# Conditioned transformer block on one core: early clearing of silu's tile, a sixth idle product, later ff gates, another bank for one modulation product

## The chip, the cores and the metric

The kernel runs on one core of one Trainium2 chip. The metric is the device time of one execution in microseconds (us); the lower, the better. The time before the change is the median of three runs.

## The reference

The input x has 2 batches of 2048 rows of 512 float32 numbers. A condition vector t of 512 numbers per batch gives six vectors per batch (shift, scale and gate, once for each of two halves of the block).

```python
emb = silu(t) @ ada_w + ada_b                  # (2, 6 * 512)
shift_msa, scale_msa, gate_msa, shift_mlp, scale_mlp, gate_mlp = split(emb, 6)
norm = ln(x) * (1 + scale_msa) + shift_msa
h = gelu(norm @ ssm_w1 + ssm_b1)               # exact gelu, 512 -> 512
x = x + gate_msa * (h @ ssm_w2 + ssm_b2)
norm2 = ln(x) * (1 + scale_mlp) + shift_mlp
hf = gelu_tanh(norm2 @ ff_w1 + ff_b1)          # 512 -> 1024
x = x + gate_mlp * (hf @ ff_w2 + ff_b2)
```

Everything is float32.

## The kernel before

**Tiles.** The 4096 rows are cut into 8 blocks of 512 rows, four to a batch. A block x_i lies in SBUF as 128 partitions x 4 pieces (c) x 512. Per block there are four large products: hA (norm times ssm_w1, class `First`), oA (times ssm_w2, added to x), hC in two groups (norm2 times ff_w1, class `Second`) and oC (times ff_w2, added to x).

**Seven products in place of eight.** Each large product is done as seven products of quarter matrices, P1 to P7 (function `group`). Their operands are quarters and sums of quarters: nS and hS for the activations, w_s and fw_s for the weights (`sums_of_first`, `sums_of_second`, four instructions each). The order is P1, P2, P6, P5, P7, P3, P4, and in the first blocks (`FIRST`) P1, P2, P5, P6, P7, P3, P4. P1, P6, P7 and P4 share one bank of PSUM, "y"; P2 has "x", P5 and P3 have "v". After a product, VectorE (DVE) takes its bank out, and only then may the next product with that bank be written.

**The order is written by hand.** `hook(hooks, places, ops)` hangs other work behind a product; it is issued on its engine right after that product's additions. [...]

**Pools.** PSUM has a pool `ps_g` with two buffers for each of the tags x, y and v, and a pool `ps_t` with two buffers of the tag t. A new tile takes the buffer of the tile of its tag before the last, and waits until that has been read.

**The start.** SP asks, in this order, for x_0, parts 0 and 1 of ada_w, w1, part 2, w2, x_1, parts 3 and 4, the row b2 (`b2_bc`), fw1, part 5, fw2 and the row fb2. Meanwhile TensorE (PE) does `IDLE` products whose result nobody reads, and turns the small rows (condition and biases) into columns, `colsT`. ScalarE (ACT) takes silu of the condition into a tile that GpSimd (POOL) has cleared, since only 2 of its 32 columns per piece are filled (lines 578 to 584). `ada_rows(g)` then makes part g of emb with four products side by side (pada, line 158), `modulation` turns it into a column per batch (pmod), and `gates` into a row on all partitions (pgate), whose result for batch 0 stays in a ps_t buffer and is multiplied into the second weights (`weight_of_second`, the folds at line 250) and into the bias row (line 629).

**Block 0 and 1.** The norm is x times rstd plus nmr (`normal`, ACT line 348 or DVE line 352), where the statistics come from DVE (lines 315 and 316, `stats`) and rstd and nmr from POOL (`scales`, lines 324 to 335). Then it is transposed on PE in pieces k = 0 to 3 (pt, line 377) and modulated (`modulate`: ACT line 391 or DVE line 393). Around the change, the order of PE is:

- hA_0, with pada_2 behind P2 and the gates of part 2 behind P6;
- oA_0, with pada_3 and pada_4 behind P2 (`conditioning`, which also issues the norm of block 1 on ACT), the two pmods behind P6, and pt_1_0 to pt_1_3 behind P7, P3, P4 and P4;
- hA_1, with pada_5 behind P6 and the transposes of the second norm of block 0 (pt_0_0 to pt_0_3) behind P3 and P4;
- the gates of part 5, and then hC_0, hC_1 and so on in the main loop.

On POOL, the biases of x (line 495), the sums of w2 and the scales of block 1 follow the multiplied row of line 629.

Of the kernel before, what the change touches and what calls it, by code (L numbers as in the profile page):

```python
# [36 lines left out]
F32 = mybir.dt.float32  # L37
# [6 lines left out]
def kernel(  # L44
# [16 lines left out]
    nc = tc.nc  # L61
    P = 128
    B, N, D = x.shape
    H = fw1.shape[1]
    KD = D // P
# [20 lines left out]
    out_blk = out.flatten_outer_dims().rearrange("(i p c) d -> i p c d", p=P, c=C)  # L86

    G = 32
    IDLE = 5


    R_COND, R_ADA = 0, B * KD
# [58 lines left out]
    load_row(b2_bc, b2)  # L151
    fw1_sb = load_w("fw1", fw1)

    def ada_rows(g, bias=None):

        pa = ps_g.tile([P, D], F32, tag="x", name=f"pada_{g}")
        for k in range(KD):
            nc.tensor.matmul(  # L158
                pa[k * G : (k + 1) * G, :],
                silu[:, k, :],  # L160
                ada[g][:, k, :],
                start=True,
                stop=True,
                tile_position=(0, k * G),
            )
        t = work.tile([P, D], F32, tag="tmp", name=f"adarows_{g}", bufs=4)
        if bias is None:
            nc.scalar.activation(t, pa, AF.Identity)
        else:
            nc.vector.tensor_tensor(t, pa, bias, ALU.add)  # L170
        return t
# [16 lines left out]
    gate = {}  # L188

    def gates(g, b, sums_g):  # L190

        pg = ps_t.tile([P, D], F32, tag="t", name=f"pgate_{g}_{b}")
        nc.tensor.matmul(pg, pick_bc[:, b, :], sums_g, start=True, stop=True)
        gate[g, b] = pg
        if b:
            gate[g, b] = work.tile([P, D], F32, tag="gate", name=f"gate_{g}_{b}", bufs=2)
            nc.scalar.activation(gate[g, b], pg, AF.Identity)
# [47 lines left out]
    def weight_of_second(w_sb, s, gt, engs):  # L245

        K = w_sb.shape[1]

        def fold(k):
            engs[k % len(engs)].tensor_tensor(w_sb[:, k, :], w_sb[:, k, :], gt, ALU.mult)  # L250

        ops = [lambda k=k: fold(k) for k in range(K)]
        lo, hi = w_sb[:, : K // 2, :], w_sb[:, K // 2 :, :]
        q = {
            "11": lo[:, :, : D // 2],
            "12": lo[:, :, D // 2 :],
            "21": hi[:, :, : D // 2],
            "22": hi[:, :, D // 2 :],
        }
        s = thirds(s)  # L260
        return second_operands(q, s), ops + sums_of_second(q, s, nc.gpsimd)
# [31 lines left out]
    def hook(hooks, places, ops):  # L293

        for n, op in enumerate(ops):
            hooks.setdefault(places[min(n, len(places) - 1)], []).append(op)
# [249 lines left out]
    def run(ops):  # L546
        for op in ops:
            op()
# [5 lines left out]

    minus_half = const.tile([P, C], F32, tag="minus_half", name="minus_half")
    nc.gpsimd.memset(minus_half, -0.5)

    unread = small.tile([P, C], F32, tag="unread", name="unread", bufs=1)
    nc.scalar.activation(unread, minus_half, AF.Silu)
# [4 lines left out]

    idle = ps_g.tile([P, C, P], F32, tag="v", name="idle")
    for n in range(IDLE):
        if n == IDLE - 1:
            nc.tensor.transpose(pt[:, :ROWS], rows, ident[:ROWS, :ROWS])
        nc.tensor.matmul(
            idle, ident, ident.unsqueeze(1).to_broadcast([P, C, P]), start=True, stop=True  # L570
        )
# [3 lines left out]
    nc.vector.tensor_copy(colsT, pt[:, :ROWS])  # L575


    silu = const.tile([P, KD, G], F32, tag="silu", name="silu")
    nc.gpsimd.memset(silu, 0.0)
    nc.scalar.activation(  # L580
        silu[:, :, :B].rearrange("p k b -> p b k"),
        colsT[:, R_COND:R_ADA].rearrange("p (b k) -> p b k", b=B),
# [40 lines left out]
    found = {}  # L623
# [22 lines left out]
    hook(hooks, ("P1",), [n1[1].scales] + hA_sums[:2])  # L646

    def conditioning():
        rows_3, rows_4 = ada_rows(3), ada_rows(4)
        for c in range(C):  # L650
            n1[1].normal(c, on_pe=True)
        found.update(shift=rows_3, scale=rows_4)

    hook(hooks, ("P2",), hA_sums[2:] + [conditioning])
    hook(hooks, ("P6",), [lambda: modulation(3, 0, found["shift"]), lambda: modulation(3, 1, found["scale"])])
    hook(hooks, ("P7", "P3", "P4"), n1[1].turned((3,)))
    n2 = {0: Norm(0, 2)}
    st = n2[0].stats()
    hook(hooks, ("P3",), st[:2])
# [1 line left out]
    fw1_ops, fw1_sums = weight_of_first("fw1", fw1_sb)  # L661
    run(fw1_sums)
    run(n1[1].summed(nc.vector))
    run(st[2:])

    hooks = {}
    hook(hooks, ("P1",), [n2[0].scales])
    hook(hooks, ("P2",), [lambda c=c: n2[0].normal(c, on_pe=True) for c in range(C)])
    hook(hooks, ("P2",), biases(1, gb[2]))
    hook(hooks, ("P6",), [lambda: found.update(rows=ada_rows(5, brows[:, 1, :]))])  # L670
    hook(hooks, ("P3", "P3", "P4", "P4"), n2[0].turned((1, 3)))
    hA[1] = First(1, n1[1].ops, hooks, FIRST)
    for b in reversed(range(B)):
        gates(5, b, found["rows"])
    fw2_ops, fw2_fold = weight_of_second(fw2_sb, fw2_s, gate[5, 0], (nc.vector,))
    n2_sums = n2[0].summed(nc.vector, nc.gpsimd)
    run(n2_sums[:2])
    fb2_bc = work.tile([P, D], F32, tag="gb", name="gb5_0", bufs=2)
# [1 line left out]
    load_x(2)  # L680
    gb[5] = fb2_bc

    def gb5_0():
        nc.vector.tensor_tensor(fb2_bc, gate[5, 0], fb2_bc, ALU.mult)

    first_hooks = {}
    hook(first_hooks, ("P1", "P2"), n2_sums[2:])
    hook(first_hooks, ("P6", "P5", "P7", "P3"), fw2_fold[:4])
    fold = None


    for i in range(NBLK):
        nxt, nx2, last = i + 1 < NBLK, i + 2 < NBLK, i + 1 == NBLK
        if nx2:
            n1[i + 2] = Norm(i + 2, 1)

        hooks = {} if i else first_hooks
        if nxt:
            hook(hooks, EARLY if i else ("P2",), hA[i + 1].summed(nc.gpsimd))
        if nx2:  # L700
            hook(hooks, ("P2", "P3", "P4"), n1[i + 2].stats())
        if fold:
            hook(hooks, ("P5", "P7"), fold[:2])
        hC = Second(i)
        hC.group(0, n2[i].ops, hooks)

        hooks = {}
        if nx2:
            hook(hooks, ("P1",), [n1[i + 2].scales])
            hook(hooks, EARLY, [lambda c=c: n1[i + 2].normal(c) for c in range(C)])  # L710
            hook(hooks, ("P7", "P3", "P3", "P4"), [lambda c=c: n1[i + 2].turn(c) for c in range(C)])
            hook(hooks, ("P4",), [n1[i + 2].move])
        hook(hooks, EARLY, hC.summed(0, nc.gpsimd))
        if i == 0:
            hook(hooks, ("P1", "P2", "P6", "P5"), fw2_fold[4:8])
            hook(hooks, ("P7",), fw2_fold[8:] + [lambda: gb5_0(), lambda: run(biases(0, gb[5]))])
        if fold:
            hook(hooks, EARLY, fold[2:6])
        hC.group(1, n2[i].ops, hooks)

        hooks = {}
        hook(hooks, EARLY, hC.summed(1, nc.gpsimd))
        if nxt:
            if nx2:
                hook(hooks, ("P7",), n1[i + 2].moved())
            if fold:
                hook(hooks, EARLY, fold[6:8])
                hook(hooks, ("P7",), fold[8:])
            n2[i + 1] = Norm(i + 1, 2)
            hook(hooks, ("P3", "P4"), n2[i + 1].stats())  # L730
            residual(f"oA_{i + 1}", i + 1, hA[i + 1], w2_ops, KD // 2, hooks)
        else:
            for p in EARLY:
                run(hooks.get(p, ()))
        fold = None

        hooks = {}
        if nxt:
            hook(hooks, ("P1",), [n2[i + 1].scales] + [lambda c=c: n2[i + 1].normal(c) for c in range(C)])
            hook(hooks, ("P2", "P2", "P6"), [lambda c=c: n2[i + 1].turn(c) for c in range(C)])  # L740
            hook(hooks, ("P6",), [n2[i + 1].move])
        if i + 3 < NBLK:
            hook(hooks, ("P6",), [lambda: load_x(i + 3)])
        refold2 = (i + 2) % PER_B == 0 and nx2
        if refold2:
            hook(hooks, ("P1",), [lambda: load_w("w2", w2, w2_sb)])
        if nx2:
            if refold2:
                gb[2] = gate_bias(gate[2, (i + 2) // PER_B], b2, "gb2_1")
            hook(hooks, ("P1", "P2"), n1[i + 2].summed(nc.gpsimd))  # L750
            hook(hooks, ("P2", "P6"), biases(i + 2, gb[2]))
        if nxt:
            hook(hooks, ("P3",), n2[i + 1].moved())
        hook(hooks, ("P3",), [lambda: store(i, 0)])
        residual(f"oC_{i}", i, hC, fw2_ops, KH // 2, hooks, last)
        if not last:
            store(i, 1)
        if nxt:
            run(n2[i + 1].summed(nc.gpsimd))

        refold5 = (i + 1) % PER_B == 0 and nxt
        if refold5:
            load_w("fw2", fw2, fw2_sb)
            gb[5] = gate_bias(gate[5, (i + 1) // PER_B], fb2, "gb5_1")
            fw2_ops, fold = weight_of_second(
                fw2_sb, fw2_s, gate[5, (i + 1) // PER_B], (nc.vector,)
            )
        hooks = {}
        if nxt:
            hook(hooks, EARLY, biases(i + 1, gb[5]))  # L770
        if refold2:
            w2_ops, w2_fold = weight_of_second(w2_sb, w2_s, gate[2, (i + 2) // PER_B], (nc.gpsimd,))
            hook(hooks, ALL, w2_fold)
        if nx2:
            hA[i + 2] = First(i + 2, n1[i + 2].ops, hooks)
        else:
            for p in ORDER:
                run(hooks.get(p, ()))
# [45 lines left out]
```

## Time and profile before

| what | value |
|---|---|
| runs | 629.41, 629.85, 634.3 us |
| median | 629.85 us |
| profiled execution, its own time | 633.62 us |
| its span, first to last instruction | 631.5 us |
| mean granted PE clock | 0.986 of full |
| PE, DVE, ACT, POOL busy | 97%, 46%, 28%, 57% |
| HBM read, written | 25.20 MB, 8.39 MB |

The profiled execution is one run, and its own time is 2.1 us more than its span. Engine names are those of the profile: PE for products, PEld for loading their weights, DVE, ACT and POOL, and SP, which issues most of the transfers. "x<-y" is the tile written and the tile read. In a wait line the figures are the total in us, how often, and the longest. In a line of a stretch stand its length, each engine's busy time with the number of instructions, the granted PE clock, the busy share of the DMA engines, and GB/s. A timeline line has start, duration, engine, line of the kernel and operation, and in brackets how long the engine stood idle before it and what ended that.

### The profile page before, as it was taken

What the parts mean: (1) busy time and instruction counts of PE and PEld (TensorE: products, weight loads), DVE (VectorE), ACT (ScalarE), POOL (GpSimd) and SP (SyncE); (2) the same over time, 40 slices, a digit from 0 to 9 for tenths busy, and PEclk for the clock granted to TensorE, in tenths of its full rate; (3) what the DMA queues carried; (4) which work ended last, traced back from release to release, by engine and by line L of the source; (5) the groups of instructions that cost most, each with busy time, mean ns of one, the idle gap of its engine ahead of it and who ended that gap; (6) DMA issues with size and microseconds to landing.
All of it is one profiled execution on the core that took longest, in us unless ns stands there. A gap on an engine that the chain in (4) does not pass through costs nothing.

```text
span 631.5 us, 7734 instructions
## 1 busy us (share of the span) xinstructions
PE 615.3 (97%) x2835; PEld 528.7 (84%) x2835; DVE 292.8 (46%) x492; ACT 176.1 (28%) x264; POOL 359.5 (57%) x376
## 2 busy tenths in 40 slices
PE   6999899999999999999999999999999999997997
PEld 2768688888888888888888888888888888886886
DVE  3486586534553355433455357533555233532321
ACT  2223513314422333214123324115223222012110
POOL 3277459949437457358957259976455383314430
PEclk8799999999999999999999999999999999999999
DMA  8951001042021501433020640224010400012001
GB/s 328 417 221 68 0 2 46 22 109 92 1 68 37 163 0 27 125 86 114 1 63 21 183 153 8 60 58 142 1 50 18 134 1 0 1 38 96 1 0 67
DMA packets 22057, 47.72 MB, mean 76 GB/s; under 512 B 4052, under 2 KB 4608, under 8 KB 21124
## 3 DMA queue, kind: packets, MB, share of 16 engines
q1 hardware_dynamic: 21936, 47.20, 23.6%
q8 instruction: 22, 0.36, 0.2%
q14 instruction: 15, 0.12, 0.1%
q10 hardware_dynamic: 84, 0.03, 0.0%
HBM read 25.20 MB, written 8.39 MB: 53 GB/s over the span
## 4 chain that ended last, share of the span: by engine, by line
PE 94%; DVE 2%; DMA 1%; POOL 1%; ACT 0%; issue 0%; DVEq 0%; SPq 0%
PE py_oC L278 18%; PE py_hC L278 17%; PE pv_hC L278 9%; PE py_oA L278 9%; PE pv_oC L278 9%; PE py_hA L278 9%; PE pv_oA L278 4%; PE px_oC L278 4%; PE pv_hA L278 4%; PE px_hC L278 4%; PE px_oA L278 2%; PE px_hA L278 2%; PE pada L158 1%; PE pt L377 1%; PE pmod L181 1%; DMA x<-in_x_dram 1%
## 5 line engine op out<-in xcount | busy, mean ns | idle before, releaser
L495 POOL TENSOR_TENSOR x<-x,gb 128x512 f32<-128x512 f32 x64 | 79.8, 1281 | 15.1 <-issue 15.1
L391 ACT ACTIVATE nT<-nT,mod,mod 128x512 f32<-128x512 f32 x52 | 38.1, 802 | 171.8 <-DMA nT<-blocks 159.9
L278 PE MATMUL py_hC<-nS,fw_s 128*128 128x256 f32 x256 | 61.3, 383 | 2.2 <-POOL nS L219 2.2
L217 POOL TENSOR_TENSOR nS<-nT 128x512 f32<-128x512 f32 x13 | 16.5, 1272 | 79.7 <-ACT nT L391 46.4
L348 ACT ACTIVATE nT<-x,nmr,rstd 128x512 f32<-128x512 f32 x52 | 38.7, 803 | 68.9 <-POOL nmr L335 68.9
L278 PE MATMUL py_oC<-fw_s,hSC 128*128 128x256 f32 x256 | 57.9, 379 | 0.0
L278 PEld LDWEIGHTS py_hC<-nS,fw_s 128*128 128x128 f32 x256 | 48.8, 191 | 9.3 <-POOL nS L219 2.6
L278 PEld LDWEIGHTS py_oC<-fw_s,hSC 128*128 128x128 f32 x256 | 48.6, 190 | 6.6
L482 DVE TENSOR_TENSOR x<-py_oC,x 128x512 f32<-128x512 f32 (+1 forms) x33 | 22.2, 672 | 60.5 <-PE py_oC L278 60.1
L324 POOL TENSOR_SCALAR ve<-mv 128x4 f32<-128x4 f32 x16 | 4.3, 268 | 75.7 <-DVE mv L316 69.2
L315 DVE BATCH_NORM_STATS2 st<-x 128x6 f32<-128x512 f32 x64 | 43.1, 674 | 5.1 <-DMA x<-in_x_dram 4.8
L207 POOL TENSOR_TENSOR hSC<-hClo 128x512 f32<-128x512 f32 x16 | 20.4, 1273 | 29.4 <-ACT hClo L431 29.4
L359 DVE STREAM_TRANSPOSE blocks<-nT 128x512 f32<-128x512 f32 x52 | 34.0, 688 | 5.7 <-ACT nT L348 5.7
L482 DVE TENSOR_TENSOR x<-py_oA,x 128x512 f32<-128x512 f32 x32 | 22.1, 691 | 26.5 <-PE py_oA L278 25.7
L278 PE MATMUL py_hC<-nT,fw 128*128 128x256 f32 x128 | 30.6, 381 | 1.3 <-ACT nT L391 1.3
L278 PE MATMUL py_hA<-nS,w_s 128*128 128x256 f32 x128 | 30.4, 381 | 0.9 <-DVE s1hA L436 0.9
L278 PE MATMUL pv_hC<-nT,fw 128*128 128x256 f32 x128 | 31.2, 388 | 0.0
L278 PE MATMUL py_oA<-w_s,hSA 128*128 128x256 f32 x128 | 30.3, 380 | 0.0
L278 PE MATMUL pv_hC<-nT,fw_s 128*128 128x256 f32 x128 | 30.2, 379 | 0.0
L278 PE MATMUL py_hC<-nS,fw 128*128 128x256 f32 x128 | 30.2, 379 | 0.0
L278 PE MATMUL px_hC<-nT,fw 128*128 128x256 f32 x128 | 30.2, 379 | 0.0
L278 PE MATMUL py_oC<-fw_s,hChi 128*128 128x256 f32 x128 | 29.2, 380 | 0.5 <-DVE x L482 0.5
(146 smaller groups left out, 1255.2 us busy)
## 6 DMA issues: line engine op xcount, KB each, us to landing
nT<-blocks SPq DMA_DIRECT2D x208, 64.0 KB, 2.0
out_dram<-x SPq DMA_DIRECT2D x15, 512.0 KB, 7.5
x<-in_x_dram SPq DMA_DIRECT2D x7, 1024.0 KB, 6.9
ada<-in_L_cond_ada_w_dram SPq DMA_DIRECT2D x6, 1024.0 KB, 11.9
fw<-in_L_cond_ff_w_dram SPq DMA_DIRECT2D x3, 2048.0 KB, 15.1
w<-in_L_cond_ssm_w_dram SPq DMA_DIRECT2D x3, 1024.0 KB, 6.8
x<-in_x_dram SPq DMA_DIRECT2D x2, 512.0 KB, 4.6
gb<-in_L_cond_ssm_b_dram SPq DMA_DIRECT2D x2, 256.0 KB
```

Source lines behind the costliest of these rows:

```text
L158: nc.tensor.matmul(pa[k * G : (k + 1) * G, :], silu[:, k, :], ada[g][:, k, :], start=True, stop=True, tile_position=(0, k * G),)
L181: nc.tensor.matmul(pv[:, n, :], sums_g[:, n * P : (n + 1) * P], pick, start=True, stop=True)
L207: lambda: eng.tensor_tensor(s[1], q["11"], q["21"], ALU.subtract),
L217: lambda: eng.tensor_tensor(s[1], q["22"], q["12"], ALU.subtract),
L278: nc.tensor.matmul(ps[b][:, j, :], lhs(p, j, k), rhs(p, j, k), start=(fresh and j == 0 and k == 0), stop=(p in ("P2", "P3", "P4") and k == ...
L315: nc.vector.bn_stats(st, xs[self.i][:, c, :])
L348: nc.scalar.activation(t, x_c, AF.Identity, bias=self.nmr[:, c : c + 1], scale=self.rstd[:, c : c + 1])
L359: nc.vector.transpose(self.bl[:, :, :, c, :].rearrange("p m k q -> p k m q"), self.nT[:, c, :].rearrange("p (k m q) -> p k m q", k=KD, m=C),)
L377: nc.tensor.transpose(pt[:, c * P : (c + 1) * P], self.xn[:, c, k * P : (k + 1) * P], ident)
L391: nc.scalar.activation(dst, src, AF.Identity, bias=shift, scale=scale)
L482: nc.vector.tensor_tensor(d, ps[BANK[p]][:, js], d, ALU.add)
L495: lambda c=c: nc.gpsimd.tensor_tensor(xs[i][:, c, :], xs[i][:, c, :], gb, ALU.add)
```

## The change

Six places are edited. The tile of silu is cleared on POOL right behind `minus_half`, ahead of the scales of block 0, instead of behind them. One more idle product is issued; the transposition of the rows stays behind the fourth, so that two stand behind it. The product of ada part 4 goes to a buffer of `ps_t` instead of the tag x of `ps_g`. The fourth modulation of block 1's first norm goes from DVE to ACT. The last two statistics of block 0's second norm move from in front of hA_1 to behind P1 of hA_1, ahead of the scales. The gates of part 5, and the making of the list of fw2's folds, move from in front of hC_0 to behind its P1. The folds themselves keep their places.

```diff
-    IDLE = 5
+    IDLE = 6
...
-    def ada_rows(g, bias=None):
-
-        pa = ps_g.tile([P, D], F32, tag="x", name=f"pada_{g}")
+    def ada_rows(g, bias=None, pa=None):
+
+        if pa is None:
+            pa = ps_g.tile([P, D], F32, tag="x", name=f"pada_{g}")
...
     nc.gpsimd.memset(minus_half, -0.5)
+    silu = const.tile([P, KD, G], F32, tag="silu", name="silu")
+    nc.gpsimd.memset(silu, 0.0)
...
-        if n == IDLE - 1:
+        if n == IDLE - 2:
             nc.tensor.transpose(pt[:, :ROWS], rows, ident[:ROWS, :ROWS])
...
-    silu = const.tile([P, KD, G], F32, tag="silu", name="silu")
-    nc.gpsimd.memset(silu, 0.0)
...
-        rows_3, rows_4 = ada_rows(3), ada_rows(4)
+        rows_3 = ada_rows(3)
+        rows_4 = ada_rows(4, pa=ps_t.tile([P, D], F32, tag="t", name="pada_4"))
...
-    hook(hooks, ("P7", "P3", "P4"), n1[1].turned((3,)))
+    hook(hooks, ("P7", "P3", "P4"), n1[1].turned())
...
-    run(st[2:])
...
-    hook(hooks, ("P1",), [n2[0].scales])
+    hook(hooks, ("P1",), st[2:] + [n2[0].scales])
...
-    for b in reversed(range(B)):
-        gates(5, b, found["rows"])
-    fw2_ops, fw2_fold = weight_of_second(fw2_sb, fw2_s, gate[5, 0], (nc.vector,))
+
+    def ff_gate():
+        for b in reversed(range(B)):
+            gates(5, b, found["rows"])
+        found["fw2"] = weight_of_second(fw2_sb, fw2_s, gate[5, 0], (nc.vector,))
+
...
+    def fold5(lo, hi):
+        return [lambda k=k: found["fw2"][1][k]() for k in range(lo, hi)]
...
+    hook(first_hooks, ("P1",), [ff_gate])
     hook(first_hooks, ("P1", "P2"), n2_sums[2:])
-    hook(first_hooks, ("P6", "P5", "P7", "P3"), fw2_fold[:4])
+    hook(first_hooks, ("P6", "P5", "P7", "P3"), fold5(0, 4))
...
-            hook(hooks, ("P1", "P2", "P6", "P5"), fw2_fold[4:8])
-            hook(hooks, ("P7",), fw2_fold[8:] + [lambda: gb5_0(), lambda: run(biases(0, gb[5]))])
+            hook(hooks, ("P1", "P2", "P6", "P5"), fold5(4, 8))
+            hook(hooks, ("P7",), fold5(8, 12) + [gb5_0] + biases(0, gb[5]))
...
+        if i == 0:
+            fw2_ops = found["fw2"][0]
```

## The prediction

> **What bounds the kernel now.** I read the page first, then the waits of PE (who it waited for), then the timeline of the first 80 us, and last the busy table over chosen stretches, whose third column from the right is the granted PE clock.
>
> ```profile
> span 631.5 us, 7734 instructions
> PE 615.3 (97%) x2835; PEld 528.7 (84%) x2835; DVE 292.8 (46%) x492; ACT 176.1 (28%) x264; POOL 359.5 (57%) x376
> PEclk8799999999999999999999999999999999999999
> ...
> PE pada L158 <- ACT silu L580: 3.2, 1, 3.2
> ...
> PE pada L158 <- DVE x L482: 1.4, 1, 1.4
> ...
> PE py_hA L278 <- DVE s1hA L436: 0.9, 1, 0.9
> PE pgate L193 <- ACT nT L391: 0.7, 1, 0.7
> ```
>
> PE is busy 97% of the span, and from 80 us to 570 us it waits for nobody. Only the start has waits that this change touches: the four shown, 6.2 us. The clock row says the start is also slow (8, 7). The stretches show how:
>
> ```profile
> 8.09:11.50 3.41, 0.43 (x2) 0.00 (x0) 0.88 (x7) 0.01 (x1) 2.67 (x9) 1.00 1.05 393
> 11.50:14.91 3.41, 2.43 (x11) 0.70 (x11) 0.85 (x2) 1.36 (x3) 0.58 (x1) 0.50 1.05 408
> ...
> 21.74:25.15 3.41, 3.41 (x13) 3.05 (x12) 2.44 (x5) 1.53 (x2) 0.00 (x0) 0.50 1.05 408
> 42.20:45.60 3.40, 2.03 (x19) 0.47 (x17) 3.37 (x4) 0.60 (x1) 3.24 (x3) 1.00 0.00 0
> ...
> 578.10:581.52 3.42, 1.26 (x6) 1.00 (x6) 0.69 (x1) 0.63 (x1) 3.26 (x3) 1.00 0.00 0
> 581.52:584.93 3.41, 3.41 (x10) 2.68 (x9) 0.69 (x1) 0.00 (x0) 3.41 (x4) 0.50 0.00 0
> ```
>
> After a stretch of 3.41 us with 0.43 us of PE work the clock halves, for four stretches (11.50 to 25.15); after one with 1.26 it halves for one; after one with 2.03 (the two pada products with the 1.4 us wait between) it stays full. So the 3.2 us wait for silu costs itself and then half speed through the whole first stage. The lines that price the steps, from the timeline and from the view of the tile ada:
>
> ```profile
> 11.25 0.20 POOL L579 MEMSET silu<- 128x128 f32 x1
> 11.49 0.22 ACT L580 ACTIVATE silu<-colsT 128x8 f32<-128x8 f32 x1 [3.47 <-POOL silu L579]
> 11.76 1.93 PE L158 MATMUL pada<-ada,silu 128*32 128x512 f32 x8 [3.24 <-ACT silu L580]
> ...
> 33.87 0.67 DVE L629 TENSOR_TENSOR gb<-pgate,gb 128x512 f32<-128x512 f32 x1
> 34.68 4.97 POOL L495 TENSOR_TENSOR x<-x,gb 128x512 f32<-128x512 f32 x4 [15.05 <-issue]
> ...
> 49.60 2.93 ACT L348 ACTIVATE blocks<-x,nmr,rstd 128x512 f32<-128x512 f32 x4 [2.75 <-POOL nmr L335]
> 53.19 0.60 PE L377 MATMUL pt<-ident,blocks 128*128 128x128 f32 x4
> ...
> DMA to landing us min/median/max: 7.2/11.9/15.4
> ```
>
> **The Trainium skill.** "TensorE: Matmul & The Clock Gate", Part 1, says that the array runs at half clock by default and after an idle window, at full clock after a busy one, that a window is 3413 ns, and that it runs free, so its phase differs from run to run. The trace agrees: the clock changes at 11.50, 25.15, 581.52 and 584.93 us, all whole multiples of 3.41 apart. That also explains two kinds of run: 629.41 and 629.85 against 634.3, the profiled one (633.62) being of the second kind. The same page, under "Architectural detail", has ACT, DVE and POOL as strict first-in-first-out queues; here px_oA's addition (L482), whose product had ended by 42.8, starts at 44.39, behind L207 and L208 on DVE. "DMA: Bandwidth & Descriptors", "Queues, rings and completion order": on each DMA engine descriptors are taken in ring order, so a row asked for behind nine large loads comes after them. The first four pieces of ada's landings agree (8.8, 11.6, 16.7, 24.3 us, in the order of issue).
>
> **Part 1, silu cleared early and a sixth idle product.** Before: nmr ends 11.31, memset 0.20, silu 0.22, pada at 11.76. After: POOL has nothing between 2.2 and 8.2 us, so the memset is free; silu follows colsT (ends 8.21) at about 8.27 and ends at 8.5. PE holds the second idle product behind rowsT: 0.86 us at full clock (two passes of 0.43, the spacing of the weight loads at 4.81 to 5.67), so it is free at 9.1. The first piece of ada lands at 1.63 + 7.2 = 8.8. So pada starts at 9.1 and takes 1.07 (the full-clock row at 27.69, against 1.93). ACT 0.60: 10.8; pmod 0.92 (half of 1.84 for x16): 11.7; second pada (its ada lands at 11.6): 12.8. The transposes now wait for nmr, unmoved at 11.31, plus two ACT normals of 0.75: 12.9. Then pt 1.0, pmod 0.95, pt 1.0: P1 of hA_0 at 15.8 instead of 23.14. Its w1 landed by 14.33. In the stretch 8.09 to 11.50 PE now has about 2.7 us of work, over the 2.03 that kept the clock, so I take the clock as full. For a run before with a full clock the same sum gives P1 at 18.45 and, with P1 at full speed as well (1.0 us), 5.7 us less than the profiled run; the runs show 3.8 to 4.9 less.
>
> **What is late next: b2.** L629 multiplies the row b2_bc by the gate. From P1 it comes 9.7 us later at full clock: 25.5. But b2_bc is asked for behind ada 4, whose issue began at 14.40 - 2.90 = 11.5 and landed 15.4 later, at 26.9; 256 KB at 410 GB/s add 0.6: 27.5. So DVE stands 2.0 us at L629. Queued behind it are the w2 folds and P7's addition; they had 1.0 us of room before P4, so PE stands about 1.0 there. POOL is the longer chain: from L629 its biases, the w2 sums and the scales lead to the end of ACT's normals at 52.53, 18.66 after L629. After: 27.5 + 18.66 = 46.2.
>
> **Part 2, own bank for ada part 4.** The 1.4 us wait for px_oA's addition goes: pada_4 follows pada_3. Its new slot was held by the ssm gate, last read by the folds (37.8 before, 31 after), 5 us ahead. But pt_1_0 needs the normals: PE would be there at about 44.1 and they end at 46.2. So pt_1_0 ends at 46.3 against 53.79: parts 1 and 2 give 7.5 us against the profiled run, 1.8 against a full-clock run (where pt_1_0 would end at 48.1). The bank alone is worth 0.6 of its 1.4, the slack between 52.53 and 53.19.
>
> **Part 3, hA_1: statistics behind P1's addition, fourth modulation on ACT.** L217 waits for ACT (59.72 instead of DVE's 59.41): +0.3. s1hA then starts at 62.6 instead of 63.92, and P6 at once at 63.74: 0.9 less. Back comes: the last aggregate ends 0.9 later, so nmr and the four normals end at 71.0 instead of 70.1, while pt_0_0 would now be reached at 70.4. Net 0.35 (bounds 0 and 0.9).
>
> **Part 4, the ff gates behind P1 of hC_0.** The 0.73 us wait for the transposes' bank is covered by P1 (1.73), which needs only modulations 0 and 1, done at 73.3. The two gate products cost 1.8 wherever they stand. ACT's gate copy and table load (0.6 + 1.28) end before P2's gelu. L219 comes 1 us before P6. Net 0.75 (bounds 0.4 and 0.9). The folds keep their places, and SP's queue its order.
>
> **Sum.** 7.5 + 0.35 + 0.75 = 8.6: the profiled execution (span 631.5, 2.1 around it, 633.62) would be 625.0. Against the two full-clock runs (mean 629.6): 1.8 + 0.35 + 0.75 = 2.9, or 626.7. My model makes the half clock about 1.2 us too dear, so I stand between: **626.0 us**, 0.6% under the median of 629.85. What a measurement of this kernel can tell from no change is about 1%, 6.3 us.
>
> **Rivals.**
> - *The row is no bound* (chance 0.11). If b2_bc lands by 25.5, L629 does not wait and pt_1_0 ends at 44.4: 1.9 less, 624.1. For: its landing is not shown, only worked out from ada's. Against: DMA is saturated (393 to 410 GB/s) up to 40 us.
> - *The new wait before pt_1_0 halves the clock once* (0.15). It empties about 2 us of a stretch; 3.4 - 2.0 = 1.4 us of work lies between 1.26 (halved) and 2.03 (kept). One stretch at half speed is 1.7: 627.7. For: 581.52. Against: the stretches have to fall on it.
> - *The first stage still runs at half clock* (0.12): pada and pmod may count for little (the stretches from 14.91 to 21.74 are full of such work and didn't raise the clock). Then P1 comes at 18.9, L629 at 29.7, 2.2 after the row: 628.2. Against: 42.20 to 45.60.
> - *Slower* (0.04): the new wait before pt_1_0 halves the clock, and the pieces of transposes there keep it so for four stretches, as from 11.50 to 25.15. Price 5.6: 631.6. It decides from 4 us lost on, three stretches. Against: P3 and P4 stand between those transposes, and the stretch with P1 in it (21.74) raised the clock.
>
> **Numbers.** Forecast 0.58, its own range 624.6 to 627.4. The range for 8 in 10 takes in the first two rivals and most of the third: 623.8 to 628.5. Faster by over 1% (below 623.6, or a comparison in which most runs before had the slow start): 0.17. Within 1%: 0.79. Slower by over 1%: 0.04, the last rival.
>
> **What would show it.** In the changed profile: silu near 8.3 and pada near 9.1 without a wait for ACT; clock 1.00 from 11.5 to 25; P1 of hA_0 near 16; L629 held by the DMA of gb near 27.5; a wait of about 2 us of pt for ACT's blocks near 46; no waits of pada for L482, of py_hA for s1hA, of pgate for nT. I am wrong if the clock is 0.50 in the first stage, if L629 starts near 25.5 without a DMA, or if hA_1 or hC_0 shows a new wait of over 1 us.

## The result and the profile after

Over ten runs of each, the changed kernel takes 626.92 us (624.87 to 627.35) and the kernel before 631.69 us (629.41 to 634.3). The ratio is 0.9918, with a 95% interval of 0.9893 to 0.9942: 0.8% faster, which is clear of no change but under 1%. The median of before rose from the 629.85 of its first three runs because most of the later runs were longer; what makes them so is the granted clock, as the part on the prediction works out. The profiled execution of the changed kernel has a span of 624.5 us and a time of its own of 626.36 us, against 633.62 us.

From the page of the changed kernel, the span, PE's busy time and the row of PE's clock:

```profile
span 624.5 us, 7738 instructions
PE 612.0 (98%) x2837; PEld 525.5 (84%) x2837; DVE 295.1 (47%) x491; ACT 176.5 (28%) x265; POOL 359.4 (58%) x376
...
PEclk9999999999999999999999999999999999998999
```

The clock's 8 and 7 at the start are gone. The 8 near the end is a stretch of half clock that before had too, at 581.52, spread there over two slices; it comes up again below. From the waits of PE in the changed kernel (who was waited for; total, times, longest):

```profile
PE py_hC L279 <- POOL nS L220: 2.2, 1, 2.2
PE py_hA L279 <- DVE s5hA L448: 1.5, 1, 1.5
...
PE pt L378 <- ACT blocks L349: 1.1, 3, 0.4
...
PE py_hA L279 <- DVE u2hA L443: 0.4, 1, 0.4
```

The four waits of before (pada for silu, pada for px_oA's addition, py_hA for s1hA, pgate for nT) are gone. Smaller ones have come in their place: P4 of hA_0 waits 1.5 us for an addition on DVE, the first transposes of block 1 wait 0.8 us for ACT and those of block 0's second norm 0.3 (1.1 in all), and P7 of hA_1 waits 0.4 us for P6's addition. The first line, 2.2 us, belongs to the last block and was there before. From the timeline of the changed kernel:

```profile
8.46 0.22 ACT L581 ACTIVATE silu<-colsT 128x8 f32<-128x8 f32 x1 [0.73 <-DVE colsT L578]
9.97 1.07 PE L159 MATMUL pada<-ada,silu 128*32 128x512 f32 x8
...
16.69 1.99 PE L279 MATMUL py_hA<-nT,w 128*128 128x256 f32 x8
...
29.17 0.69 DVE L630 TENSOR_TENSOR gb<-pgate,gb 128x512 f32<-128x512 f32 x1 [2.31 <-DMA gb<-in_L_cond_ssm_b_dram]
...
31.71 1.99 PE L279 MATMUL py_hA<-nS,w 128*128 128x256 f32 x8 [1.49 <-DVE s5hA L448]
...
44.84 2.93 ACT L349 ACTIVATE blocks<-x,nmr,rstd 128x512 f32<-128x512 f32 x4 [5.16 <-POOL nmr L336]
```

silu runs at once behind colsT, pada no longer waits and takes 1.07 us in place of 1.93, and hA_0 starts 6.5 us earlier. Then DVE stands 2.31 us for the transfer of the row b2: the row starts only 4.7 us earlier than before. From the view of the tile ada in the changed kernel, where the largest figure is that of part 4, asked for just ahead of the row (15.4 in before):

```profile
DMA to landing us min/median/max: 7.4/12.1/16.8
```

Part of what PE had gained beyond that goes into the new waits: P4 of hA_0 starts 5.7 us earlier (31.71 in place of 37.42).

### The profile page after: what moved, and what is told of

Its sections match the earlier page's. It is cut to its first block, busy times and chain, and to the rows that moved or that the text cites. A ratio compares the mean times of both kernels' runs of the same rounds, so it can differ in the third digit from the quotient of the medians.

```text
span 624.5 us, 7738 instructions
## 1 busy us (share of the span) xinstructions
PE 612.0 (98%) x2837; PEld 525.5 (84%) x2837; DVE 295.1 (47%) x491; ACT 176.5 (28%) x265; POOL 359.4 (58%) x376
## 4 chain that ended last, share of the span: by engine, by line
PE 92%; POOL 3%; ACT 1%; DVE 1%; issue 1%; DMA 0%; POOLq 0%; SPq 0%
PE py_oC L279 18%; PE py_hC L279 18%; PE pv_hC L279 9%; PE pv_oC L279 9%; PE py_oA L279 8%; PE py_hA L279 8%; PE px_oC L279 4%; PE pv_oA L279 4%; PE px_hC L279 4%; PE pv_hA L279 4%; PE px_oA L279 2%; PE px_hA L279 2%; PE idle L572 1%; ACT blocks L349 1%; PE pt L378 1%
## 5 line engine op out<-in xcount | busy, mean ns | idle before, releaser
L279 PE MATMUL py_oC<-fw_s,hChi 128*128 128x256 f32 x128 | 29.2, 380 | 0.5 <-DVE x L483 0.5
```

The source lines that it names most:

```text
L279: nc.tensor.matmul(ps[b][:, j, :], lhs(p, j, k), rhs(p, j, k), start=(fresh and j == 0 and k == 0), stop=(p in ("P2", "P3", "P4") and k == ...
```

## The experiments

All timelines can be set side by side at the same marks. The table gives the start in us of P1 of hA_0, of the multiplied row, of P3 of oA_0 (right behind pt_1_0), of P1 and P4 of hA_1, and of P2 of hC_0, and the time from there to the end of the span. It is one profiled execution each. The last two columns are the median and the ends of all runs, and the times of those runs whose mean granted clock is given as 1.000 ("full clock" below).

| kernel | hA_0 P1 | row | oA_0 P3 | hA_1 P1 | hA_1 P4 | hC_0 P2 | rest | runs: median (ends) | at clock 1.000 |
|---|---|---|---|---|---|---|---|---|---|
| before | 23.14 | 33.87 | 53.63 | 58.39 | 71.98 | 79.02 | 552.48 | 631.69 (629.41 to 634.3) | none |
| changed | 16.69 | 29.17 | 47.99 | 52.76 | 66.16 | 72.21 | 552.29 | 626.92 (624.87 to 627.35) | 624.87, 625.01 |
| p1_only | 16.24 | 28.98 | 47.80 | 52.57 | 66.59 | 73.63 | 553.07 | 628.29 (626.58 to 628.87) | 626.58 |
| warm_only | 20.11 | 29.94 | 49.69 | 54.46 | 68.05 | 75.08 | 552.92 | 627.28 (626.27 to 630.14) | 626.27, 626.71 |
| silu_late | 22.37 | 32.72 | 51.61 | 56.38 | 69.79 | 75.83 | 550.67 | 628.32 (627.27 to 628.37) | none |
| idle5 | 15.80 | 29.11 | 48.67 | 53.44 | 66.54 | 72.59 | 552.81 | 626.84 (626.62 to 627.24) | none |
| b2_late | 15.84 | 33.47 | 53.03 | 57.80 | 70.92 | 76.97 | 552.33 | 631.09 (629.8 to 632.47) | none |
| b2_early | 16.33 | 26.55 | 45.42 | 50.19 | 63.61 | 69.66 | 550.84 | 622.60 (622.4 to 624.12) | 622.40, 622.48, 622.73 |
| no_bank | 15.95 | 28.93 | 50.02 | 54.78 | 67.89 | 73.94 | 550.66 | 626.34 (624.86 to 628.96) | 624.86 |
| b2_early_no_bank | 16.85 | 26.75 | 46.50 | 51.27 | 64.36 | 70.41 | 551.09 | 623.14 (622.59 to 624.17) | 622.59, 622.87 |
| no_part3 | 16.67 | 29.12 | 47.93 | 52.70 | 66.70 | 72.75 | 550.55 | 625.63 (625.48 to 627.6) | 625.48, 625.59 |
| no_part4 | 16.74 | 29.21 | 48.02 | 52.78 | 66.19 | 73.22 | 550.68 | 626.89 (625.74 to 628.36) | 625.74, 625.79 |
| b2_scales | 16.86 | 26.84 | 45.05 | 49.82 | 63.25 | 69.30 | 552.30 | 621.80 (621.5 to 623.51) | 621.50, 621.58, 621.80 |
| b2_scales_idle5 | 17.34 | 27.16 | 45.40 | 50.17 | 63.60 | 69.65 | 552.95 | 623.38 (621.26 to 627.25) | 621.26, 621.55 |

The rest varies by 1.7 us with a stretch of half clock near the end that some executions have and others don't. Parts worth less than that are therefore read from the marks and from the runs at full clock, and not from the medians. The ratios below are to the runs of before that belong to each experiment. Their medians are 632.84 to 633.67, where the result above has 631.69, so these ratios are not to be set against each other.

**Part 1 alone, on the kernel before.**

```diff
-    IDLE = 5
+    IDLE = 6
...
     nc.gpsimd.memset(minus_half, -0.5)
+    silu = const.tile([P, KD, G], F32, tag="silu", name="silu")
+    nc.gpsimd.memset(silu, 0.0)
...
-        if n == IDLE - 1:
+        if n == IDLE - 2:
...
-    silu = const.tile([P, KD, G], F32, tag="silu", name="silu")
-    nc.gpsimd.memset(silu, 0.0)
```

> The kernel before with part 1 alone (silu's tile cleared early, sixth idle product). Theory (part 1 carries nearly all, through the silu wait and the clock): the clock is full from about 7 us on in every run, hA_0 starts near 16.7 us, the row of L629 waits for b2_bc near 29 us, and the time is 627.5 to 628.5 us with a spread under 2.5 us (the changed kernel less about 0.3 for pada_4's bank and 1.1 for parts 3 and 4). Rival (the later parts carry half): 629.5 us or more.

Measured: 628.29 us, ratio to before 0.9919 (0.9892 to 0.9946), within the expected band. The clock is full through the first stage, hA_0 starts at 16.24 and the row waits until 28.98 for its transfer. Part 1 carries 5.4 of the 6.8 us that hC_0's P2 moves (79.02 to 73.63, and on to 72.21).

**Eight idle products, silu still late.**

```diff
-    IDLE = 5
+    IDLE = 8
...
-        if n == IDLE - 1:
+        if n == IDLE - 4:
```

> The kernel before with eight idle products in place of five, four of them behind the transposition of the rows, and nothing else: silu stays late, so PE has work while it waits. Theory (the half clock costs 4 to 5 us, and the two kinds of run before differ by it): clock 1.00 in the first stage, hA_0 starts near 18.5 us in place of 23.1, all runs at 629.0 to 630.0 us, none near 634. Rival (the clock follows the late silu only, or its cost is covered by the wait for b2_bc): runs still spread from 629 to 634.

Measured: 627.28 us, ratio 0.9929 (0.99 to 0.9959), and better than expected: no run is near 634. So the half clock cost more than the expectation had put on it. The expectation took runs of 629 to 630 us for runs of before at full clock; the two runs here that had it took 626.27 and 626.71, no more than the 626.58 of p1_only. The expectation that the clock would be 1.00 throughout failed in the profiled run, the longest of the seven. PE's wait for silu is down to 0.6 us, and yet one stretch runs at half speed. The stretches before and after the change of clock (columns as in the prediction):

```profile
11.15:14.56 3.41, 2.12 (x19) 1.14 (x19) 1.00 (x2) 1.86 (x4) 0.43 (x3) 1.00 1.05 404
14.56:17.98 3.42, 3.42 (x17) 1.76 (x17) 0.17 (x1) 0.95 (x2) 3.26 (x3) 0.50 1.05 410
```

2.12 us of PE work did not keep the clock, though the kernel before kept it with 2.03 at 42.2. All but 0.06 of that work is pada (32 of 128 columns) and pmod (2 moving columns). In these records a stretch's busy time doesn't decide by itself.

**silu late in the changed kernel.** The two lines that clear silu's tile go back behind colsT; the sixth idle product stays.

> The changed kernel with silu's tile cleared late again, six idle products kept. Theory (one more product covers the wait only in part: PE is idle from about 9.4 to 11.8 us): the wait of pada for silu is 2 to 2.5 us, the clock may halve for one or more stretches between 11 and 25 us, hA_0 starts at 18.5 to 22 us, and with parts 3 and 4 kept the time is 627 to 630 us, more spread than the changed kernel. Rival (the clearing is worth nothing, since b2_bc bounds the start): 627 us with no half clock.

Measured: 628.32 us. PE waits 2.1 us for silu, and the clock is at half from 13.4 to 23.6:

```profile
9.97:13.38 3.41, 1.06 (x8) 0.16 (x8) 1.00 (x2) 0.60 (x2) 1.18 (x6) 1.00 1.03 389
13.38:23.62 10.24, 9.98 (x43) 8.07 (x44) 2.04 (x5) 3.74 (x6) 5.08 (x4) 0.50 1.04 413
```

hA_0 starts at 22.37 and hC_0's P2 3.6 us later than in the changed kernel. The median is 1.4 us higher; in the profiled execution 1.6 us of the 3.6 are made up in the rest, by the stretch at the end that it lacks. With six idle products the early clearing is what matters: one more product does not bridge the wait. Eight did so in most runs of warm_only, with silu still late. What counts is that DVE comes to the row by the time that b2 has landed, near 29, and the early clearing is one way to that.

**The sixth idle product undone.** `IDLE = 5`, one product behind the transposition.

> The changed kernel with five idle products, one behind the transposition of the rows (the sixth undone). Theory (silu is ready at 8.7 us and part 0 of ada_w lands at 9.0, so the sixth product only fills time): the first pada starts at 9.0 to 9.3 us, the clock is full until the wait for b2_bc, the row starts when it did, and the time is within 0.5 us of 626.9. Rival (the sixth product is what keeps the clock): half clock between 11 and 15 us, and 1 to 3 us more.

Measured: 626.84 us, no different from the changed kernel. pada starts at 9.10 (it waits 0.6 us for part 0 of ada_w) and hA_0 at 15.80, 0.9 us earlier, but the row starts at 29.11, as in the changed kernel: b2's transfer hides the sixth product. The clock is full through the first stage here too, without that product; behind the wait for the row it is at half for one stretch (31.9 to 35.3), and hA_1 starts 0.7 us later than in the changed kernel. What the sixth product is for shows only where that cover is gone, in b2_scales_idle5 below.

**The row b2 asked for earlier, and later.**

```diff
     load_x(1)
+    b2_bc = work.tile([P, D], F32, tag="gb", name="gb2_0", bufs=2)
+    load_row(b2_bc, b2)
     load_ada(3)
     load_ada(4)
-    b2_bc = work.tile([P, D], F32, tag="gb", name="gb2_0", bufs=2)
-    load_row(b2_bc, b2)
     fw1_sb = load_w("fw1", fw1)
```

> The changed kernel with the row b2_bc asked for ahead of parts 3 and 4 of ada_w. Theory (b2_bc's landing bounds the start): the multiplied row starts near 26.9 us in place of 29.2, PE's wait of 1.5 us at P4 of hA_0 is gone, the norm of block 1 ends 2.3 us earlier, and the time falls by 1.5 to 2.3 us, to 624.6 to 625.4. Rival (POOL's and ACT's chain has other bounds): the wait at P4 moves into the wait for the transposes of oA_0, and the time falls by under 0.5 us.

Measured: 622.60 us, ratio 0.9843 (0.9808 to 0.9878). The row starts at 26.55, behind the statistics on DVE and no transfer:

```profile
26.55 0.67 DVE L630 TENSOR_TENSOR gb<-pgate,gb 128x512 f32<-128x512 f32 x1
```

The wait at P4 is gone, pt waits 0.7 us in place of 1.1, and hC_0's P2 comes 2.55 us earlier (72.21 to 69.66), 0.3 over the upper end expected. The median falls by 4.3; 1.5 us of the difference between the two profiled executions is the half clock at the end, which this one lacks. At full clock three runs took 622.40 to 622.73 us, against 624.87 and 625.01: 2.4 us, as the marks say. In b2_late, the two lines stand behind fw1.

> The changed kernel with the row b2_bc asked for behind the 2 MB of fw1, which take about 5.1 us. Theory: the multiplied row starts near 34.2 us in place of 29.2, the wait at P4 of hA_0 grows by 5 us to 6.5, and the time rises by 5 us, to about 632, slower than before. Rival (the row is covered): under 1 us more.

Measured: 631.09 us over 20 runs, ratio to before 0.9981. The row starts at 33.47 and the wait at P4 is

```profile
PE py_hA L279 <- DVE s5hA L448: 6.4, 1, 6.4
```

as expected (6.5). The row moved by 4.3 us, hC_0's P2 by 4.8 and the median by 4.2. The wait also cost clock: it is at half from 32.5 to 39.3. So the landing of a 256 KB row bounded the changed kernel's start, in both directions.

**pada_4's bank undone**, with the row late and with it early: `ada_rows(4)` again.

> The changed kernel with the product of ada part 4 back in the tag x of ps_g (part 2 undone). Theory (the norm of block 1 bounds oA_0, so the bank is worth nothing while b2_bc is late): pada waits about 1.0 us for px_oA's addition again, the transposes no longer wait for ACT, pt_1_0 ends 19.0 us after the multiplied row starts, as with the bank, and the time is within 0.3 us of the changed kernel's 626.9. Rival (the prediction's 0.6 us): pt_1_0 ends 19.6 us after the row, 627.5.

Measured: 626.34 us. The profiled execution is no clean comparison: behind the wait for the row its clock halved for one stretch.

```profile
28.42:31.84 3.42, 1.44 (x7) 0.93 (x7) 2.91 (x5) 0.39 (x1) 2.08 (x2) 1.00 1.02 417
31.84:35.25 3.41, 3.41 (x10) 2.67 (x9) 2.91 (x7) 1.26 (x4) 3.41 (x4) 0.52 1.05 410
```

From the row to P3 of oA_0 it takes 21.09 us. With the bank and the same half clock (idle5) it is 19.56, with the bank and full clock (changed) 18.82, and without the bank and with full clock (p1_only) 18.82 too. So at full clock and with the late row the bank is worth nothing (the one run at clock 1.000, 624.86, says the same), and where half a clock has put PE behind, 1.5 us at that mark, from one trace each.

> The changed kernel with b2_bc early but pada_4 back in the tag x of ps_g. Theory (the bank saves PE time, but only what the norm of block 1 leaves): pada waits 1.0 to 2.0 us for px_oA's addition, the 0.7 us wait of the transposes goes, hA_1 starts 0.4 to 0.9 us later than with the bank (50.2), 623.2. Rival (worth nothing here too): within 0.2 us of 50.2.

Measured: 623.14 us. pada waits 1.4 us, and from the row to hA_1 it takes 24.52 us in place of 23.64: 0.9, at the upper end. The bank saves PE time, of which the norm of block 1 leaves a part, or none. By hC_0's P2 0.75 of it is left (70.41 against 69.66), and the two runs at full clock lie only 0.2 above those of b2_early, so how much of it reaches the time is not shown.

**Part 3 undone.** `turned((3,))`, and `run(st[2:])` back in front of hA_1.

> The changed kernel with the fourth modulation of block 1 back on DVE and the last two statistics back in front of hA_1 (part 3 undone). Theory from the two traces: P1 to P4 of hA_1 takes 14.0 us in place of 13.4, the time rises by 0.6 to 627.5. Rival (the prediction's 0.35, with the rest given back by the late norm): 13.75 us, 627.2. Second rival (part 3 costs, by the wait of the transposes for the norm): under 13.4.

Measured: hA_1 takes 14.00 us from P1 to P4 in place of 13.40, with a wait of 1.3 us for s1hA. hC_0's P2 is 0.5 later. The median of these four runs, 625.63, is 1.3 under that of the changed kernel all the same; the profiled one lacks the half clock at the end (1.7), so the medians don't settle a part of this size. At full clock two runs took 625.48 and 625.59 us, against 624.87 and 625.01: 0.6, as the marks say. Against before, the gain by the marks is less: there hA_1 took 13.59, with 0.9 of wait. In p1_only it takes 14.02 as well.

**Part 4 undone.** `ff_gate()` in front of hC_0.

> The changed kernel with the ff gates back in front of hC_0 (part 4 undone). Theory from the two traces: P4 of hA_1 to P2 of hC_0 takes 7.05 us in place of 6.05, PE waits 0.7 us for the fourth transpose's bank again, and the time rises by 1.0 to 627.9. Rival (the prediction's 0.75): 6.8 us, 627.7.

Measured: from P4 of hA_1 to P2 of hC_0 7.03 us in place of 6.05, with the wait back:

```profile
PE pgate L194 <- ACT nT L392: 0.7, 1, 0.7
```

The median is 626.89, and at full clock the two runs are 0.8 above those of the changed kernel. By the marks part 4 is worth 1.0 us: the 0.7 of the wait, 0.15 until the first gate product is under way, and 0.1 of the gates themselves, which take 1.71 us behind a running product and 1.82 behind a gap.

**A better version.** b2 early, and the scales of block 1 ahead of w2's last sum:

```diff
-    hook(hooks, ("P7",), fold2(2, 8))
+    hook(hooks, ("P7",), fold2(2, 7))
...
-    hook(hooks, ("P1",), [n1[1].scales] + hA_sums[:2])
+    hook(hooks, ("P1",), [n1[1].scales] + fold2(7, 8) + hA_sums[:2])
```

> The changed kernel with b2_bc asked for ahead of parts 3 and 4 of ada_w, and the scales of block 1 on POOL ahead of the last of w2's four sums (which P4 of oA_0 alone needs). Theory (with the row early, the norm of block 1 still ends 0.7 us behind PE): nmr ends 1.6 us earlier, the transposes don't wait for ACT, hA_1 starts at 49.4 to 49.6 us in place of 50.2, and the time is 0.6 to 0.8 us under the same kernel with the row alone (622.6), near 621.9. Rival (the last sum is late for P4, or POOL and DVE get in each other's way): no gain or a new wait at P4 of oA_0.

Measured: 621.80 us, ratio to before 0.9829 (0.9807 to 0.9852), the best of all. From the row to hA_1 it takes 22.98 us in place of b2_early's 23.64, and pt no longer waits in oA_0. hA_1 starts at 49.82, later than expected; hA_0 started 0.5 later here and the row 0.3. At full clock the time is 0.9 under b2_early's.

> The same with five idle products in place of six. With the row out of the way the 0.87 us that the sixth product holds PE should show: theory, hA_0 starts 0.5 to 0.9 us earlier and so does all that follows, the clock stays full, about 621.3. Rival (part 0 of ada_w or the norm of block 0 comes next): hA_0 starts under 0.3 us earlier. Second rival (the sixth product keeps the clock in some runs): some runs 1.7 us or more slower.

Measured: 623.38 us, from 621.26 to 627.25. The second rival holds: pada starts 1.1 us earlier (9.02), and hA_0 0.5 later (17.34), since the clock halves between:

```profile
8.80:12.21 3.41, 2.48 (x20) 1.31 (x24) 0.94 (x3) 1.42 (x3) 2.06 (x7) 1.00 1.04 395
12.21:15.62 3.41, 3.41 (x20) 2.36 (x12) 0.26 (x2) 1.30 (x2) 1.26 (x1) 0.50 1.05 408
```

A pada product, a pmod and the start of a second pada make up the 2.48 us of the first stretch, and do not count for enough. The best run of these two kernels is this one's, and so is the worst: the sixth product buys no time of its own (at full clock five products are about 0.2 faster), but the runs suggest that it makes the clock safer. That is six runs against five and one trace.

## Why the prediction was right, and where it was off

The forecast of 626.0 stood 0.9 us under the measured median. In the profiled executions, 8.6 us had been worked out and 7.26 came: to P3 of oA_0 5.64 in place of 7.5; part 3 0.19 in place of 0.35; part 4 0.99 in place of 0.75; and 0.45 in the rest and outside the span, which was not predicted and is no part of the change that I can name.

- *Part 1* held in mechanism: silu at 8.46 (8.27 was said), pada without a wait, clock full. hA_0 came 0.9 later than worked out, since the idle products kept the slow pace for longer in this execution (their weight loads were still 0.85 us apart at 6.62, and 0.43 from 4.81 on in that of before) and so ended later. I take this for the clock; the profile's column has 1.00 there in both. The row hid that.
- *What is late next: b2* held, and is the step that was mis-sized. The row started at 29.17, not 27.5. I had put the landing at part 4 of ada_w plus its bytes; in six executions with b2 in this place and an early first stage it came at 28.9 to 29.2. The 1.7 us are most of the 1.9 missing. The term that was off is the landing of part 4, taken over from the kernel before. Its issue began at 11.63 and it took 16.8 us (the line of the tile ada above), so it landed at 28.4 in place of 26.9: 1.5 of the 1.7 us. In those six executions it took 16.7 to 17.0 us to land, against 15.4 in before, and the row started 0.7 to 0.8 behind it, close to the 0.6 worked out from its bytes. Why part 4 itself landed later is not shown: the transfers moved 385 to 431 GB/s in stretches of 4 us from 4 to 40 us, and 387 to 424 in before (393 to 410 was said).
- *From the row on* the chain through POOL and ACT was as worked out: 15.6 us from the row to nmr's end (15.7 before).
- *Part 2*: 0.6 was forecast as the slack left by the norm. With the row late it is 0.0 (p1_only against the changed kernel), and with the row early 0.9 at hA_1's P1. The reason given, that the norm bounds oA_0, is what the two runs show.
- *Part 3*: inside the bounds; the norm did come late, and pt_0_0 waited for it (0.3).
- *Part 4* was over its upper bound of 0.9, by the gates' own gap, which I had counted as equal in both places.
- *The two kinds of run before*: right that the clock makes them, but there are not two kinds, and none is at full clock. The 45 runs of before that were taken beside the experiments have mean granted clocks of 0.986 to 0.995, and their times follow: 21 of 0.986 or 0.987 took 633.3 to 634.6 us, 13 of 0.989 took 632.0 to 633.3, 6 of 0.992 took 630.9 to 631.6, and the 5 of 0.995 took 629.2 to 629.5. In the traces 0.986 is five stretches of half clock (before), and 0.995 is two (idle5, warm_only). By their times, the runs that I called full-clock, 629.41 and 629.85, had about two such stretches; their own clocks are not on record. So the gap of 3.8 to 4.9 us is about three stretches and not all of them, and the step "My model makes the half clock about 1.2 us too dear" rested on a comparison that was not there. At 0.995 the five runs of the changed kernel took 626.9 to 627.4 us, about 2 us under those of before; the rest of the gain in the medians is that the changed kernel has fewer stretches at half clock. That 626.0, put between 625.0 and 626.7 on that step, came so near the median was in part luck.
- *Rivals*: the half clock behind a new wait did come, but behind the wait for the row (no_bank, idle5, b2_late) and not at pt_1_0. That pada and pmod count for little was held against one stretch that kept its clock; warm_only and b2_scales_idle5 show it to be so in others. It didn't decide here: the clock stayed full in the first stage of the changed kernel's profile. That the sixth idle product held it is not shown, since idle5 kept it without that product.

## What to carry to other kernels

When a wait at the start of a kernel is removed, work out from the bytes in the queue when each transfer lands, and ask which small one stands behind large ones: here a 256 KB row behind nine megabytes cost 2.4 us, and asking for it two transfers earlier recovered them. Leave room in that sum: the landing of the transfer ahead of it moved by 1.5 us from one kernel to the other. A wait of PE is to be priced with the clock it costs afterwards, and that differs from run to run (seven runs of warm_only had 0.994 to 1.000). Look at the granted clock of every run before you take a median, or a short run, for the kernel at full clock. Part values under that spread are read from marks in the timelines and from runs of like clock, and an edit's worth depends on which chain is ahead at the time.

## What the runs showed of the hardware that I had not expected

- A PE stretch of 3.41 us can be 73% busy by its records (2.48 us in b2_scales_idle5) and the clock still halves, when the work is products of 32 columns and of two moving columns; another with 2.03 us (before, at 42.20), of which 0.56 were full products, kept it. So did 8.00 to 11.41 of idle5, with the same products as b2_scales_idle5 but shifted, and 0.54 us of an idle product in it: 2.15 us in all. Where the border lies was not measured, nor was it tested apart from what else differs.
- A half-clock stretch near the end, behind the 2.2 us wait of the last block, comes in some executions and not in others, though that wait is there in thirteen of the fourteen traces. The time from hC_0's P2 to the end is 550.55 to 550.84 us in the five traces without any half clock there and 552.29 to 553.07 in the eight with it: 1.7 us, the half of one stretch. In b2_early_no_bank (551.09) that stretch fell earlier, from 567.2 to 570.6, and the wait of 2.2 us was only 0.5.
